# Layer 1's expert matrices: three certain blocks' loads go to other buffers, and the later blocks' places follow

## The chip, the core and the metric

The kernel runs on one core of a Trainium2 chip. The core has five engines with an instruction queue each: TensorE (PE, with its weight loads shown apart as PEld), VectorE (DVE), ScalarE (ACT), GpSimd (POOL) and SyncE (SP). 16 DMA engines move data between memory and the core's on-chip memory. The metric is device time in microseconds; the time before is the median of 8 runs, 1903.46 us (1897.4 to 1906.86).

## What is computed

Four layers over 2708 rows of 256 numbers. Each layer adds a product with the adjacency matrix, then a feed-forward part. The change lies in layer 1's feed-forward part, a mixture of 8 experts of which each row goes to one:

```python
H = gelu(layernorm(x) @ W1 + b1)            # 2708 x 1024
probs = softmax(H @ Wg + bg)                # 2708 x 8
assign = argmax(probs)
for e in range(8):
    y = H @ Wd[e] + bd[e]                   # 1024 x 256 matrix of the expert
    out += where(assign == e, probs[:, e] * y, 0)
x = x + out
```

## The kernel before

*Blocks.* Which expert a row goes to is known only on the chip. Rows of H are kept in memory (`hid`), and each row's number and weight are scattered to a place sorted by expert (`taken`). Every 128 places of one expert are a block. Layer 1 runs 24 blocks always, at positions 0 to 23. Positions 0 to 8 are the NA = 9 certain ones: blocks that are full by the first two of three groups of row tiles (2048 rows), taken in the order of the experts and run in thirds (0, 3, 6, 1, 4, 7, 2, 5, 8). Positions 9 to 23 are the ALWAYS = 15 rest blocks, in the order of the list REST1, whose pairs are (block of the rest, buffer). Should the data need more, a branch after position 17 (L1467, `all_again`) computes them; with these inputs its body isn't run, but every engine passes the branch.

*One position* (`Units`, L687 to 830). POOL gathers the 128 names from `taken` (L551), then their rows of `hid` into one of four tiles `hs` (L693). PE turns the rows (L708, 8 transposes, through `ps_acc`), ACT copies them to `hTs` (L709), PE multiplies with the expert's matrix `wb` into `yacc` (L781, 16 instructions), DVE adds the bias, a part of `wb` too (L784), and scales (L785), and POOL scatters the rows to `given` (L537). PE turns the next position's rows ahead of a position's product. At the last certain position (8) it is otherwise: the transposes of position 9 stand two products before the end of position 8's, those of position 10 right behind them.

*Matrices.* A matrix with its bias is 128 x 2304 floats (1152 KB, `L1_ffn_Wdp`). `weights1` loads it through SP's queue into one of six buffers `wb`, numbered 0 to 5. SP first reads the block's expert from on-chip memory (L564). A buffer remembers the expert it was loaded with, and the load (L1170) carries a condition: it moves nothing if the expert is the same. The issue waits for the buffer's last reader, DVE's bias addition. SP works in order, so what is queued behind a waiting issue waits too. Buffers 0 to 2 lie in a pool of their own (`w1`); buffers 3 to 5 are in a pool (`w1r`) that opens when the gate's pool is closed, in its room. `fetch` keeps two matrices ahead for the certain positions; `fetch_rest` keeps up to three ahead for the rest, and asks for none whose buffer is still to be read.

Before, the certain positions use buffers 0, 1, 2 in turn (position b uses b % 3), and so the loads of positions 6, 7 and 8 follow the reads of positions 3, 4 and 5. The rest starts with buffers 3, 4 and 2.

*What comes behind.* The rows of `given` are read back by SP (`load_tiles`, L56) as `mine`, and added to x by DVE and POOL (L1587). Layer 2 begins with transposes (L1592), their copies (ACT, L1594) and a projection (L267). Its pool `t3` lies in the room of layer 1's, among it the constants that POOL loads (L127 Wr, L121, L1530, L1532, L1537). The builder orders each engine's instructions; waits follow from which tiles share room.

Of the kernel before, what the change touches and what calls it, by code (L numbers as in the profile page):

```python
# [49 lines left out]
def load_tiles(nc, dst, tiles, src, first=0):  # L50

    done = []
    full = [t for t in tiles if rows(t) == P]
    if full:
        t0, m = full[0], len(full)
        done.append(nc.sync.dma_start(  # L56
            dst[:, t0 - first : t0 - first + m, :],
            src[t0 * P : (t0 + m) * P, :].rearrange("(t p) d -> p t d", p=P)))
    for t in tiles:
        if rows(t) < P:  # L60
            done.append(nc.sync.dma_start(dst[: rows(t), t - first, :],
                                          src[t * P : t * P + rows(t), :]))
    return done
# [3 lines left out]
def adj_ffn4(ctx: ExitStack, tc: tile.TileContext, a: dict, out: bass.AP):  # L67
# [64 lines left out]
    def pin(last=None):  # L132

        pinned.append(tc.keep_in_program_order(
            s.preload_act_table_set("natural_log_exp_and_others")))
        if last is not None:
            tc.add_manual_dep(pinned[-1].ins, last, mybir.DependencyInfo(
                mybir.DependencyClass.NoSync, mybir.DependencyReason.DATA), reason="table")
# [405 lines left out]
    def behind(i, past):  # L544
        for p in past:
            tc.add_manual_dep(i.ins, p.name, mybir.DependencyInfo(
                mybir.DependencyClass.Sync, mybir.DependencyReason.DATA), reason="scattered rows")
# [114 lines left out]
    class Units(Blocks):  # L662
# [72 lines left out]
        def fetch_rest(self):  # L735
            while self.rest and len(self.rest_ahead) < 3:
                n, k = self.border + self.at[1], REST1[self.at[1]][1]
                if max((i for i in range(n) if buffer_of(i) == k), default=-1) >= self.now:
                    break
                self.rest_ahead.append(self.weights(self.border + self.at[1], expert_of(self.rest.pop(0))))  # L740
                self.at[1] += 1
# [128 lines left out]
    NA, MOST = 9, (2 * N + E * (P - 1)) // (2 * P)  # L870
# [5 lines left out]
    with ExitStack() as l0:  # L876
# [99 lines left out]
        for tiles in GROUPS:  # L976
# [8 lines left out]
            for j in range(FULL):  # L985
# [50 lines left out]
                if end and j == 0:  # L1036
                    items = [(early, b, past0, taken[0][: 2 * held0], True) for b in range(N0)]
# [12 lines left out]
            if end:  # L1050
# [3 lines left out]
                hc = l0.enter_context(  # L1054
                    tc.tile_pool(name="c0", side="right", reuse_waits="tile", bufs=1))
# [61 lines left out]
        for q, t0, t1 in ((P, 0, FULL), (LAST, FULL, NT)):  # L1117
            d = ps_tmp()
            for t in range(t0, t1):
# [16 lines left out]
    NA, MOST = 9, (N - E) // P + E + 1  # L1136
    assert NA <= -(-(held - E * (P - 1)) // P)
    ALWAYS, AHEAD1 = 15, 9
    EARLY, prepared = GROUPS1[0], {}

    REST1 = [(0, 3), (4, 4), (6, 2), (1, 3), (5, 4), (7, 2), (2, 3), (8, 2), (3, 3),
             (9, 5), (10, 1), (11, 4), (12, 0), (14, 2), (13, 0)]

    def buffer_of(b):

        return b % 3 if b < NA else REST1[b - NA][1]

    assert sorted(b for b, _ in REST1) == list(range(ALWAYS))
    assert all(b < AHEAD1 for b, _ in REST1[:AHEAD1])
    with ExitStack() as l1:  # L1150
# [5 lines left out]
        wbs, reads = {}, []  # L1156
# [5 lines left out]
        def weights1(b, e):  # L1162

            k = buffer_of(b)
            if k not in wbs:
                wbs[k] = [wbs["pool" if k < 3 else "more"].tile([P, 2048 + D], F32, name="wb", bufs=3),
                          None]
            wb, was = wbs[k]
            wbs[k][1] = e
            i = nc.sync.dma_start(wb, a["L1_ffn_Wdp"][bass.ds(e, 1)].rearrange("e p n -> p (e n)"),  # L1170
                                  cond=None if was is None else e != was)
            after(i, reads[-1])
            return wb.rearrange("p (f d) -> p f d", d=D)
# [180 lines left out]
        work1 = Units(hw, given[1], weights1, hid)  # L1354
        for tiles in GROUPS1:
# [83 lines left out]
            if end:  # L1439
                sums.close()  # L1440
                gnn.close()
                psum_pool(l1, 3, 3)
                wbs["pool"] = l1.enter_context(
                    tc.tile_pool(name="w1", side="right", reuse_waits="tile", bufs=1))
                hc = l1.enter_context(
                    tc.tile_pool(name="c1", side="right", reuse_waits="tile", bufs=1))
                work1.hs.append(hc.tile([P, HC * P], F32, name="hs", bufs=1))
                work1.hTs = [hc.tile([P, HC, P], F32, name="hTs", bufs=2) for _ in range(2)]
                g.memset(work1.hs[-1], 0.0)
                work1.more()  # L1450
                between = work1.pieces(hc, lambda b: beside(b), {NA + AHEAD1: lambda: branch()})
                send1(tiles, ready, between)
                break
# [9 lines left out]
        items = [(rest, b, past, taken[1], False) for b in range(MOST - NA)]  # L1463

        def branch():

            with tc.If(left[0] > 0):  # L1467
                work1.all_again(hc, items[AHEAD1:], wbs[3][0],
                                slice(NA + AHEAD1, NA + ALWAYS))
            pin(scattered["given1"][-1].name)  # L1470
            wbs[3][1] = None
            known_rows = list(scattered["given1"])
            for t0, o in zip(EARLY[::4], work1.early):
                for i in load_tiles(nc, o.rearrange("p (t d) -> p t d", d=D), range(t0, t0 + 4),
                                    given[1], t0):
                    tc.declare_no_dep(i.ins, group="given1", keep=known_rows,
                                      reason="rows of other blocks")
                    tc.add_to_no_dep_group("given1read", i.ins)
                    behind(i, known_rows)
# [6 lines left out]

        work1.add([items[b] for b, _ in REST1])
        for _ in between:
# [799 lines left out]
```

## Time and profile before

| what | us |
|---|---|
| median of 8 runs (lowest, highest) | 1903.46 (1897.4, 1906.86) |
| the profiled execution's own time | 1902.83 |
| its span, first to last instruction | 1901.1 |
| DVE busy | 1075.0 |
| ACT busy | 656.9 |
| POOL busy | 390.7 |
| first product of layer 1's blocks (L781) | 961.4 |
| end of the last one | 1088.3 |

The mean granted TensorE clock of the execution is 0.985. A line of the timeline has the start, the span, the engine, the line, the operation, what is written and read, the shape and the count; in brackets stands the idle time of the engine just before it and what ended that. "issue" means that the engine waited for nothing that the profile shows; "PEq" is PE's own instruction queue. In the table of windows the times are those from the span's start.

### The profile page before, as it was taken

To read this page: it belongs to the slowest core of one execution; us is meant where nothing else is said; L and a number is where in the kernel's file an instruction comes from. 1 tells how busy PE (TensorE), PEld (TensorE's weight loads), DVE (VectorE), ACT (ScalarE), POOL (GpSimd) and SP (SyncE) were. 2 spreads that over 40 slices of the span, in tenths; PEclk is the share of its full clock that TensorE was granted. 3 is DMA by queue.
4 is the path that set the end of the run, shared out by engine and by line. 5 is a ranking of instruction groups with operands and counts; after the bars stand their busy time and mean duration, and the time that the engine had idled before them with its cause. 6 is when DMAs were issued, how large, how long until landed. Compare 5 with 4: busy or idle time off the path is not lost. (4 is left out here: it accounts for less than half of the span.)

```text
span 1901.1 us, 25846 instructions
## 1 busy us (share of the span) xinstructions
PE 1820.5 (96%) x9453; PEld 1332.0 (70%) x9453; DVE 1075.0 (57%) x2467; ACT 656.9 (35%) x1472; POOL 390.7 (21%) x460
## 2 busy tenths in 40 slices
PE   8999998999999999999888999999899999999998
PEld 7888777888888788888777878887566733233344
DVE  7686871443433625344542365555355498888877
ACT  8777741222222302113222332322232542132232
POOL 0015353333322001403446410000000100011020
PEclk9999998999998999999989999999899999999999
DMA  8536655887773554544746452000101000012120
GB/s 267 158 99 165 228 187 210 333 333 265 289 285 101 178 151 124 126 131 122 220 134 220 171 94 18 1 1 1 44 1 34 18 1 23 23 26 37 23 37 18
DMA packets 92638, 232.81 MB, mean 122 GB/s; under 512 B 18223, under 2 KB 48983, under 8 KB 84952
## 3 DMA queue, kind: packets, MB, share of 16 engines
q1 hardware_dynamic: 70936, 184.46, 30.3%
q0 software_dynamic: 21568, 46.61, 9.0%
q8 instruction: 78, 1.28, 0.3%
q14 instruction: 56, 0.46, 0.1%
HBM read 218.39 MB, written 30.80 MB: 131 GB/s over the span
## 5 line engine op out<-in xcount | busy, mean ns | idle before, releaser
L2160 DVE SCALAR_TENSOR_TENSOR e<-arena,G,mask 128x1024 f32<-128x1024 f32 (+1 forms) x252 | 275.1, 1150 | 34.1 <-PE den L2197 33.2
L2189 PE MATMUL num<-e,wh 128*64 128x512 f32 (+4 forms) x1056 | 214.0, 549 | 0.7 <-ACT L_gnn_W L1498 0.3
L1420 PE MATMUL acc<-sup,adrow 128*128 128x256 f32 x882 | 198.5, 382 | 3.5 <-DMA adrow<-in_adjT 1.9
L1723 PE MATMUL ps_acc<-hh,e 128*128 128x257 f32 x882 | 199.2, 382 | 1.7 <-ACT o L1666 1.7
L1024 PE MATMUL acc<-msg,wt 128*128 128x256 f32 x882 | 197.9, 381 | 1.8 <-DVE wt L974 1.2
L1420 PEld LDWEIGHTS acc<-sup,adrow 128*128 128x128 f32 x882 | 164.9, 190 | 31.7 <-issue 5.5
L1024 PEld LDWEIGHTS acc<-msg,wt 128*128 128x128 f32 x882 | 165.0, 190 | 27.6 <-issue 2.1
L1723 PEld LDWEIGHTS ps_acc<-hh,e 128*128 128x128 f32 x882 | 163.7, 190 | 29.2 <-ACT o L1666 4.3
L649 PE MATMUL yacc<-wb,hTs 128*128 128x256 f32 x736 | 170.8, 384 | 6.7 <-DVE ys L651 4.0
L615 PE MATMUL ps_acc<-xTs,wa 128*128 128x256 f32 (+1 forms) x768 | 170.3, 374 | 4.2 <-DVE xTs L605 3.0
L617 ACT ACTIVATE hTs<-ps_acc,wa 128x256 f32<-128x256 f32 (+1 forms) x192 | 88.8, 465 | 247.3 <-PE yacc L649 167.1
L615 PEld LDWEIGHTS ps_acc<-xTs,wa 128*128 128x128 f32 x768 | 136.8, 190 | 31.1 <-DVE xTs L605 6.2
L649 PEld LDWEIGHTS yacc<-wb,hTs 128*128 128x128 f32 x736 | 138.5, 192 | 26.0 <-DVE ys L651 5.1
L2189 PEld LDWEIGHTS num<-e,wh 128*64 128x64 f32 (+1 forms) x1056 | 70.0, 136 | 122.8 <-issue 104.9
L1715 DVE SCALAR_TENSOR_TENSOR e<-Rb,G,mask 128x640 f32<-128x640 f32 (+2 forms) x110 | 85.0, 774 | 90.5 <-PE ps_acc L1723 90.4
L2197 PE MATMUL den<-e,wh 128*32 128x512 f32 (+4 forms) x1056 | 112.2, 545 | 0.0
L1385 DVE TENSOR_SCALAR mask<-adrow 128x1024 uint8<-128x1024 f32 (+1 forms) x66 | 41.3, 625 | 123.4 <-DMA adrow<-in_adjT 123.2
L221 ACT COPY xT<-ps_tmp 128x256 f32<-128x256 f32 x76 | 26.9, 367 | 199.9 <-PE ps_tmp L220 199.5
L781 PE MATMUL yacc<-wb,hTs 128*128 128x256 f32 x384 | 91.0, 392 | 0.6 <-DMA wb<-in_L_ffn_Wdp 0.6
L974 DVE SCALAR_TENSOR_TENSOR wt<-adrow,wt 128x640 f32<-128x640 f32 (+3 forms) x67 | 71.0, 1063 | 25.8 <-ACT wt L141 24.5
L2197 PEld LDWEIGHTS den<-e,wh 128*32 128x32 f32 (+1 forms) x1056 | 33.0, 109 | 73.7 <-issue 69.6
L537 POOL DMA_INDIRECT given<-ys,xs x46 | 65.4, 1423 | 92.0 <-DVE ys L652 77.9
(487 smaller groups left out, 2631.6 us busy)
## 6 DMA issues: line engine op xcount, KB each, us to landing
adhalf<-in_adjT SPq DMA_DIRECT2D x42, 677.0 KB
wb<-in_L_ffn_W2p SPq DMA_DIRECT2D x24, 1152.0 KB
wb<-in_L_ffn_Wdp SPq DMA_DIRECT2D x24, 1152.0 KB
wa<-in_L_ffn_W1b SPq DMA_DIRECT2D x24, 1028.0 KB
adrow<-in_adjT SPq DMA_DIRECT2D x42, 512.0 KB
adrow<-in_adjT SPq DMA_DIRECT2D x42, 320.0 KB
adrow<-in_adjT SPq DMA_DIRECT2D x21, 576.0 KB
adrow<-in_adjT SPq DMA_DIRECT2D x21, 448.0 KB
```

Source lines behind the costliest of these rows:

```text
L615: i = te.matmul(p[:, f % 2, : m * P], lhsT=w1[:, c, f * P : (f + 1) * P], rhs=xT[:, c, : m * P], start=(c == 0), stop=(c == DC - 1))
L617: s.activation(hT[:, f, : m * P], p[:, f % 2, : m * P], AF.Gelu, bias=bias[:, f : f + 1])
L649: te.matmul(q[:, k, :], lhsT=hT[:, f, k * P : (k + 1) * P], rhs=w2[:, f, :], start=(f == 0), stop=(f == HC - 1))
L781: te.matmul(q, lhsT=hT[:, f, :], rhs=w2[:, f, :], start=(f == 0), stop=(f == HC - 1))
L974: v.scalar_tensor_tensor(wt, ad, 1.0, wt, op0=ALU.is_lt, op1=ALU.mult)
L1024: te.matmul(p[:q, n - pair[0], :], lhsT=wt[:, k : k + q], rhs=msg[:r, j, :], start=(j == 0 and n == pair[0]), stop=(j == FULL - 1 and n == ...
L1420: te.matmul(p[:q, n - pair[0], :], lhsT=ad[:, k : k + q], rhs=sup[:, jj, :], start=(jj == 0 and n == pair[0]), stop=(jj == FULL - 1 and n ...
L1715: i = v.scalar_tensor_tensor(e[:r, :w], Rb[:r, c0 : c0 + w], G[:r, j, :], mask[:r, j, c0 : c0 + w], op0=ALU.max, op1=ALU.mult)
L1723: te.matmul(p[:, : D + 1], lhsT=e[:, k : k + q], rhs=hh[:, j, :], start=(j == 0), stop=False)
L2160: v.scalar_tensor_tensor(e[:, :w], slow[:, m % 2, k, :w], G[:, j, 2 * pair + k, :], mask[:, j, c0 : c0 + w], op0=ALU.max, op1=ALU.mult)
L2189: te.matmul(num[k * DK : (k + 1) * DK, hf, :q], lhsT=wh[some, j, 2 * pair + k, :DK], rhs=e[some, :q], start=(j == 0), stop=(j == FULL), ti ...
L2197: te.matmul(den[z * Q : (z + 1) * Q, :q], lhsT=wh[some, i, 2 * pair + k, DK : DK + 1] .to_broadcast([some.stop - some.start, Q]), rhs=e[so ...
```

## The change

Certain blocks 2, 5 and 8, which are run at positions 6, 7 and 8, get buffers 3, 4 and 5 in place of 0, 1 and 2. The list of the rest keeps its order of blocks and gets other buffers. The buffer that the branch's body overwrites is now 0 in place of 3.

```diff
-    REST1 = [(0, 3), (4, 4), (6, 2), (1, 3), (5, 4), (7, 2), (2, 3), (8, 2), (3, 3),
-             (9, 5), (10, 1), (11, 4), (12, 0), (14, 2), (13, 0)]
+    REST1 = [(0, 0), (4, 1), (6, 5), (1, 0), (5, 1), (7, 5), (2, 0), (8, 5), (3, 0),
+             (9, 2), (10, 4), (11, 1), (12, 3), (14, 5), (13, 3)]

     def buffer_of(b):

-        return b % 3 if b < NA else REST1[b - NA][1]
+        return (b % 3 if b < NA - 3 else b - NA + 6) if b < NA else REST1[b - NA][1]
...
-                work1.all_again(hc, items[AHEAD1:], wbs[3][0],
+                work1.all_again(hc, items[AHEAD1:], wbs[0][0],
                                 slice(NA + AHEAD1, NA + ALWAYS))
             pin(scattered["given1"][-1].name)
-            wbs[3][1] = None
+            wbs[0][1] = None
```

The first rest positions, 9 and 10, now use buffers 0 and 1, which positions 3 and 4 were the last to read; the last ones, 22 and 23, use 5 and 3 where they used 2 and 0. PE's and ACT's instructions keep their order. SP's keep theirs but for their targets, conditions and waits. On DVE a part of layer 2's first statistics, a memset (L1521) and a comparison (L1548) change places with the last two bias additions. On POOL the last but one scatter now stands ahead of the load of Wr (L127), the last scatter behind it, and the six loads L121 to L1537 behind that; before, all seven loads stood ahead of both scatters.

## The prediction

> **What bounds the kernel now.** The page's first part comes first: TensorE (PE) is busy in nearly the whole span, so a change of transfers can only win where PE stands still or runs at half clock. The table of windows over the end of layer 1 shows where that is (columns: the stretch and its span, busy us and instructions of PE, PEld, DVE, ACT and POOL, granted clock, busy share of the DMA engines, GB/s):
>
> ```profile
> PE 1820.5 (96%) x9453; PEld 1332.0 (70%) x9453; DVE 1075.0 (57%) x2467; ACT 656.9 (35%) x1472; POOL 390.7 (21%) x460
> ```
> ```profile
> 983.00:993.00 10.00, 9.46 (x35) 8.20 (x36) 1.33 (x5) 2.35 (x5) 5.56 (x6) 0.68 0.34 97
> 993.00:1015.00 22.00, 19.18 (x103) 16.30 (x101) 3.12 (x8) 3.22 (x6) 14.14 (x15) 1.00 0.98 376
> 1015.00:1052.00 37.00, 34.96 (x185) 30.80 (x186) 9.64 (x26) 9.85 (x18) 25.38 (x25) 0.95 0.43 131
> 1052.00:1062.00 10.00, 6.97 (x35) 5.88 (x34) 1.56 (x4) 2.46 (x3) 3.12 (x4) 0.96 0.84 320
> ```
>
> Two stretches have the DMA engines at 0.98 and 0.84, and PE loses 2.8 and 3.0 us in them; between 983 and 993 the engines are at 0.34. The timeline of PE tells what the first one costs:
>
> ```profile
> 1003.37 3.62 PE L781 MATMUL yacc<-wb,hTs 128*128 128x256 f32 x16
> 1007.55 2.83 PE L781 MATMUL yacc<-wb,hTs 128*128 128x256 f32 x12 [0.56 <-DMA wb<-in_L_ffn_Wdp]
> ...
> 1012.71 0.63 PE L708 MATMUL ps_acc<-ident,hs 128*128 128x128 f32 x4 [0.59 <-issue]
> 1016.77 1.12 PE L708 MATMUL ps_acc<-ident,hs 128*128 128x128 f32 x4 [3.43 <-issue]
> 1017.68 4.86 PE L781 MATMUL yacc<-wb,hTs 128*128 128x256 f32 x16
> ```
>
> One block's output (L781, x16) is position 7 at 1003.37, 8 at 1007.55, 9 at 1017.68. Undisturbed, the step is 4.33 us (999.04 to 1003.37). The next, position 10, begins at 1023.25, so three steps took 19.88 us in place of 12.99: 6.9 us are lost. Of these 0.56 + 0.59 + 3.43 = 4.58 us are gaps, and 4.86 - 3.62 = 1.24 us are the half clock that follows the last gap.
>
> Why there: the trace's packets of 9216 B (a matrix row) are 11 x 128 in this layer, so 11 of the 24 issues of L1170 move a matrix and 13 are skipped. Three come at 932 to 946, and five, of positions 6 to 10, lie end to end from 993.3 to 1014.5. The queue's own timeline has positions 6, 7 and 8 issued at 991.47, 994.93 and 998.82, each held by DVE's bias addition of position 3, 4 or 5, the last reader of the buffer it overwrites. Positions 9 and 10 follow at 1000.14 and 1001.58 into the two untouched buffers. Gathers of hidden rows issued inside that stretch land late: the one of 1001.35 after 1010.2, while that of 983.17 took until 987.6. PE's signals to the others are late there too: DVE begins the addition of position 7 at 1013.12, though PE's record of its last product ends at 1007.0; why, the trace doesn't say.
>
> **The change, part by part.**
>
> *Positions 6, 7, 8 into buffers 3, 4, 5 (moved).* The order of SP's instructions gives what each then waits for: the last gelu into the closed gates' room (ACT, over by 957.5), the stores of hidden rows (issued until 971.88, landed by 976) and older stores of POOL. All this is past when SP has issued position 5, at 981.12. I read the spacing of such issues, 0.9 us, off 931.23, 932.21, 933.05: the three go at about 982 to 984, 9 to 15 us sooner, into the stretch at 0.34. Positions 9 and 10 now overwrite buffers 0 and 1 and inherit the waits at 991.47 and 994.9, still 7 to 9 us sooner than before. The same five transfers then run from about 983 to 1005: 5 x 3.5 us (932.97 to 937.42 and its like) and some four gathers. Position 8 has its matrix before 997, not at 1007.5: the 0.56 us go. The place that is sensitive is the end of position 8, where the code puts two blocks' transposes back to back and PE needs ACT's copies at once; in steady step that place is at 1007 to 1012, after the stretch. Bounds: nothing (PE's signals to ACT come late for a reason that has nothing to do with these loads) and -6.9 us. I take -5.8 us, the 4.58 and the 1.24 that the timeline shows, since the waits end with the transfers (1014.5 and 1016.1) and gaps of the kind are absent from 1024 to 1050, where nothing but gathers moves.
>
> What is queued behind the waiting issues: on SP only later matrices and, from 1065, the loads of given rows; nobody before position 9 needs those. What the three early loads meet: the gathers of 983.17 and 989.93, for positions 7 and 8, whose transposes stand at 998 and 1002.5 and which landed at 987.6 and 994.2. They have 8 to 10 us of slack, against 3.5 us per matrix ahead of them: hidden, at most 1 us if not.
>
> A rule on the other side, beside the row of 0.34: the Trainium skill's "DMA: Bandwidth & Descriptors", section "Issuing engines are not separate DMA queues", says that transfers of all issuers run on the same 16 engines and interleave. By it the burst is only moved, and the sum of this part would be the 0.56 us alone; the row of 993 to 1015 agrees that gathers and loads slow each other (0.98), and the row of 983 to 993 says there is room.
>
> *One matrix found in place (removed).* From the reference and its inputs I worked out the rows of each expert. The nine certain blocks are of experts 0, 2, 4, 0, 2, 4, 1, 3, 5; position 18 needs expert 4, which now still lies in buffer 2: 10 transfers, not 11. It was the first of the two that fill 1052.1 to 1061.7 (8 x 0.35 us per engine, 3.5 to 4 us). In that stretch PE stands at the branch of L1467:
>
> ```profile
> 1054.97 3.62 PE L781 MATMUL yacc<-wb,hTs 128*128 128x256 f32 x16
> 1061.61 1.94 PE L708 MATMUL ps_acc<-ident,hs 128*128 128x128 f32 x8 [3.03 <-PEq L1467]
> ```
>
> PE's branch takes 6.11 us there and its code packet starts 3.7 us after it; at layer 0's branch (L658, DMA half idle) it takes 3.54 us. Bounds: nothing (the other transfer still runs, from 1053.9 on), and -4.5 us (the 3.03 gap, and 0.9 + 0.6 us of half clock in the 1.94 against 1.04 and the 4.22 against 3.62 after it). I take -1.5 us: half the gap for half the bytes, the nearer row being this branch, not layer 0's.
>
> *The end of the layer (moved).* The last positions now read buffers 5 and 3. The constants of layers 2 and 3 lie in that room, and the order of POOL's instructions shows what follows: the load of L_ffn_Wr waits for DVE's bias addition of the last block and stands ahead of the last scatter; six more loads come behind the scatter, where they were ahead of it.
>
> ```profile
> 1082.84 0.79 POOL L127 DMA_DIRECT2D L_ffn_Wr<-in_L_ffn_Wr  x1
> ...
> 1087.40 1.06 POOL L537 DMA_INDIRECT given<-xn,names  x1 [0.30 <-issue]
> 1089.47 1.03 POOL L537 DMA_INDIRECT given<-xn,names  x1 [1.02 <-DVE sc L1623]
> ```
> ```profile
> 1089.47 2.50 DMA given<-xn,names
> ...
> 1092.64 3.92 DMA mine<-given
> ```
>
> The second fence is the chain that ended last: this scatter and the load behind it are on the path, and PE waits 2.06 us for them at 1095.96. The bias addition ends 1088.79, so 0.79 us of Wr makes the scatter start at 1089.6 or later: +0.2 to +0.8, I take +0.4. The six loads (540 KB) then share the engines with 768 KB of given rows: nothing (the engines are at 0.38 from 1090 to 1117) to +4 us (512 KB took 3.92); I take nothing. ACT's first copies of layer 2 no longer wait for the last bias addition; that is worth under 0.3 us and lies before the same 2.06 us wait, so nothing. PE's order is unchanged.
>
> *Sum:* -5.8 - 1.5 + 0.4 = -6.9 us. Against the profiled execution's own 1902.83 us (span 1901.1) that is **1895.9**. The median of the runs shown is 1903.46, 0.6 above, inside their spread of 1897.4 to 1906.9.
>
> **The rivals.** About 0.2% (3.8 us) is what a measurement of this kernel can tell from no change.
>
> *A, the forecast:* from -10.8 (6.9 and 4.5 in full, +0.6) to -3.4 (the gaps go, the rest not, +1.2): 1892 to 1899.4. Chance 0.53.
>
> *B, the burst only moves.* PE's signals come late wherever matrices and gathers crowd, now at 990 to 1003; one block's slack of 3.6 us does not hide it. For it: at 993 to 1003 DMA already stood at 0.9 and more. Against: there PE lost nothing. -0.6 - 1.5 + 0.4 = -1.7: 1901.1, no change. 0.28.
>
> *C, it doesn't do what it says:* the three loads are still held (an old reader of the room that the order of instructions tells of, but late), and leave SP at 991 as before. Then +0.4 alone: 1903.2. 0.06.
>
> *D, slower, the end of the layer.* Wr ahead of the scatter (+0.8) and the six loads beside the given rows (+4) lengthen the wait of 2.06 us. It decides once the wait passes 2.7: the gap of 2.06 was followed by full clock, one of 2.72 at 289.2 by half clock, and the half clock after 3.43 us lasted 3.4 us, 1.7 lost. 0.8 + 4 + 1.7 = +6.5, with B's -2.1 for the loads: 1907.2. 0.13.
>
> A rule on the clock, in a sentence of its own: the Trainium skill's "TensorE: Matmul & The Clock Gate", "Part 1: The HAM clock gate", has the clock drop after an idle window of about 3.4 us; by it D's clock term would be nothing unless the wait nearly doubled, while the row of 2.72 us is below that.
>
> **How the numbers follow.** Forecast A, 1895.9. Faster is A: 0.53. Same is B and C: 0.34. Slower is D: 0.13. The range reaches from 1891.5 (A's low end) to 1904.5 (C and the noise of the runs): it leaves out D and a little of A.
>
> **What would show it.** Right: issues of L1170 for positions 6 to 8 at 982 to 984; no wait for wb at position 8; position 10 near 1016 to 1017 in place of 1023.25; 10 x 128 packets; a gap under 3 us at L1467; the last scatter under 1 us behind the last bias addition. Wrong: the gaps of 4.58 us at another place before 1010, or PE's wait for the given rows (the 2.06 us at 1095.96) above 2.7 us.

## The result, and the profile after

The kernel after takes 1914.15 us (median of 12 runs, 1911.13 to 1919.26), the kernel before 1904.15 us beside it (34 runs). The ratio is 1.0057, with a 95% interval of 1.0046 to 1.0068: slower by about 10 us, where 1895.9 us and a gain were forecast. The profiled execution has a span of 1910.4 us and an own time of 1912.2 us, against 1901.1 and 1902.8 before.

The transfers moved as the prediction said. The issues of positions 6, 7 and 8 stand at 980.64, 982.30 and 983.32, the five transfers run from 980.6 to 1000.0, and the layer has 10 x 128 packets of 9216 B. The table of windows of the kernel after shows it (columns as before):

```profile
983.00:993.00 10.00, 10.00 (x46) 8.83 (x46) 1.21 (x4) 2.01 (x4) 3.10 (x3) 0.84 1.00 411
993.00:1015.00 22.00, 20.58 (x111) 17.85 (x110) 3.46 (x9) 3.81 (x7) 13.83 (x14) 1.00 0.60 209
1015.00:1052.00 37.00, 28.09 (x141) 23.57 (x140) 8.08 (x22) 7.62 (x14) 24.85 (x25) 0.86 0.40 124
```

The DMA engines are full from 983 to 993 (1.00, 0.34 before) and at 0.60 after that (0.98 before). But PE's loss did not go. It lies between 1015 and 1052 now, 8.9 us of 37 against 2.0 before, where the DMA engines are only at 0.40. The timeline of PE shows the place:

```profile
1017.20 3.21 PE L781 MATMUL yacc<-wb,hTs 128*128 128x256 f32 x14
1021.62 0.59 PE L781 MATMUL yacc<-wb,hTs 128*128 128x256 f32 x2 [1.21 <-issue]
...
1023.03 0.27 PE L708 MATMUL ps_acc<-ident,hs 128*128 128x128 f32 x1 [0.70 <-issue]
1023.75 0.62 PE L708 MATMUL ps_acc<-ident,hs 128*128 128x128 f32 x2 [0.45 <-issue]
1030.13 1.11 PE L708 MATMUL ps_acc<-ident,hs 128*128 128x128 f32 x4 [5.76 <-ACT hTs L709]
```

Position 10 begins at 1017.20, 6 us ahead of before (1023.25), as forecast. Then come gaps of 1.21, 0.70, 0.45 and 5.76 us and half clock until 1034, and position 11 begins at 1031.03, 3.5 us behind before. ACT is idle in the 5.76 us: by PE's records the transposes it waits for are over at 1024.4, and ACT starts their copies at 1029.49. Such a late signal of PE is what the prediction had seen at 1013 and could not explain.

What stood still ahead of that is POOL. Its timeline in the kernel after (first fence), and its longest wait there in the kernel before (second):

```profile
983.20 1.04 POOL L693 DMA_INDIRECT hs<-hid,names  x1 [2.29 <-issue]
...
985.86 1.05 POOL L551 DMA_INDIRECT names<-taken,b_ix  x1 [0.31 <-issue]
995.87 1.02 POOL L693 DMA_INDIRECT hs<-hid,names  x1 [8.96 <-issue]
```
```profile
989.93 1.03 POOL L693 DMA_INDIRECT hs<-hid,names  x1 [3.04 <-PE yacc L781]
```

The gather of names issued at 985.86 lands at 994.2 in the trace's packets, behind the matrices; before, issued at 985.83, it had landed at 988.5. The gather of rows needs these names, and POOL works in order: it stands still for 8.96 us, and from 1002.46 to 1025.95 it runs 18 indirect transfers back to back.

At the end of the layer, before (first fence) and after (second; its last line is from the chain that ended last):

```profile
1095.96 0.63 PE L1592 MATMUL ps_tmp<-ident,x 128*128 128x128 f32 x4 [2.06 <-DVE x L1587]
...
1099.58 3.65 PE L267 MATMUL ps_acc<-w_l,xT 128*128 128x258 f32 x16
```
```profile
1092.85 0.76 POOL L127 DMA_DIRECT2D L_ffn_Wr<-in_L_ffn_Wr  x1 [2.70 <-ACT xT L1594]
1093.91 1.01 POOL L537 DMA_INDIRECT given<-xn,names  x1 [0.31 <-issue]
...
1099.90 0.63 PE L1592 MATMUL ps_tmp<-ident,x 128*128 128x128 f32 x4 [2.91 <-DVE x L1587]
...
1103.99 0.63 PE L1592 MATMUL ps_tmp<-ident,x 128*128 128x128 f32 x4 [1.72 <-DVE x L1587]
...
1105.31 0.69 PE L1592 MATMUL ps_tmp<-ident,x 128*128 128x128 f32 x4 [0.69 <-DVE mv L194]
...
1106.20 5.12 PE L267 MATMUL ps_acc<-w_l,xT 128*128 128x258 f32 x16
...
1096.65 6.48 DMA mine<-given
```

The wait of 2.06 us has become 2.91, waits of 1.72 and 0.69 us have joined it, and the 16 products that follow run in 5.12 instead of 3.65 us. The load of given rows on the chain of waits takes 6.48 us, 3.92 before.

Two stretches carry the comparison from here on. "Blocks" is the time from the layer's first L781 to the end of the last; "end" is from there to layer 2's first L1723. The difference of the two spans, +9.3 us, is -0.65 (the blocks start earlier) + 3.81 (blocks, 126.89 to 130.70) + 4.93 (end, 28.04 to 32.97) + 1.24 (all that comes behind; e10 and e15, which have the old end, show +1.6 to 1.7 there, so it is not counted to the change).

### The profile page after: what moved, and what is told of

It is laid out like the page before. It is cut to its first block, busy times and chain, and to the rows that moved or that the text cites. A ratio compares the mean times of both kernels' runs of the same rounds, so it can differ in the third digit from the quotient of the medians.

```text
span 1910.4 us, 25846 instructions
## 1 busy us (share of the span) xinstructions
PE 1821.6 (95%) x9453; PEld 1330.7 (70%) x9453; DVE 1074.1 (56%) x2467; ACT 655.4 (34%) x1472; POOL 388.3 (20%) x460
## 3 DMA queue, kind: packets, MB, share of 16 engines
q1 hardware_dynamic: 70792, 183.28, 29.5%
q8 instruction: 78, 1.28, 0.3%
## 5 line engine op out<-in xcount | busy, mean ns | idle before, releaser
L1723 PE MATMUL ps_acc<-hh,e 128*128 128x257 f32 x882 | 199.2, 382 | 1.7 <-ACT o L1666 1.7
L1723 PEld LDWEIGHTS ps_acc<-hh,e 128*128 128x128 f32 x882 | 163.7, 190 | 29.2 <-ACT o L1666 4.3
L2189 PEld LDWEIGHTS num<-e,wh 128*64 128x64 f32 (+1 forms) x1056 | 70.0, 136 | 122.8 <-issue 104.9
L781 PE MATMUL yacc<-wb,hTs 128*128 128x256 f32 x384 | 89.4, 387 | 1.2 <-issue 1.2
```

Source lines behind the costliest of these rows:

```text
L781: te.matmul(q, lhsT=hT[:, f, :], rhs=w2[:, f, :], start=(f == 0), stop=(f == HC - 1))
L1723: te.matmul(p[:, : D + 1], lhsT=e[:, k : k + q], rhs=hh[:, j, :], start=(j == 0), stop=False)
L2189: te.matmul(num[k * DK : (k + 1) * DK, hf, :q], lhsT=wh[some, j, 2 * pair + k, :DK], rhs=e[some, :q], start=(j == 0), stop=(j == FULL), ti ...
```

## The experiments

| run | kernel | blocks | end | ratio to before (95%) |
|---|---|---|---|---|
| | before / after | 126.9 / 130.7 | 28.0 / 33.0 | 1 / 1.0057 |
| e1 | after's front, before's end | 134.6 | 28.2 | 1.0044 (1.0028, 1.0059) |
| e2 | before's front, after's end | 128.5 | 32.6 | 1.0030 (1.0009, 1.0050) |
| e3 | after, constants later | 134.3 | 29.7 | 1.0048 (1.0034, 1.0062) |
| e5 | after, names 3 ahead | 117.0 | 30.6 | 0.9982 (0.9967, 0.9996) |
| e6 | before, names 3 ahead | 118.8 | 28.3 | 0.9954 (0.9937, 0.9972) |
| e7 | e1, names 3 ahead | 121.9 | 28.1 | 0.9978 (0.9964, 0.9993) |
| e17 | e3, names 3 ahead | 122.5 | 28.1 | 0.9978 (0.9962, 0.9993) |
| e10* | e6 and breaks on POOL | 114.3 | 28.5 | 0.9949 (0.9937, 0.9962) |
| e12* | e5, Wr behind the scatter | 114.1 | 29.5 | 0.9958 (0.9944, 0.9973) |
| e13* / e14* | before / after | 123.3 / 123.4 | 28.2 / 32.4 | 1 / 1.0025 (1.0013, 1.0036) |
| e15* | as e10 | 111.8 | 28.8 | 0.9953 (0.9939, 0.9966) |

Blocks and end, in us, are those of one profile each. The experiments ran on five chips, and their traces are of two kinds. In e1 to e8, e17 and e18, as in the two profiles above, PE's signals come late in places. In the runs with a star (and e9, e11, e16) the stall that this makes near 979 is absent: position 3 begins 16.1 us after the first product there, and 21.8 to 23.9 us after it in all the others but e18. The kernel before takes 1886.7 to 1889.1 us on these chips, not 1903.5 to 1905.1. Blocks and ratios are compared only within a kind. One profile's blocks are no exact measure: those of the kernel before are 126.9 us above and 123.7 in e8, which differs from it in layer 2 alone.

### The two halves alone: e1 and e2

```diff
 e1 (from after)
-             (9, 2), (10, 4), (11, 1), (12, 3), (14, 5), (13, 3)]
+             (9, 2), (10, 4), (11, 1), (12, 0), (14, 2), (13, 0)]
 e2 (from before)
-             (9, 5), (10, 1), (11, 4), (12, 0), (14, 2), (13, 0)]
+             (9, 5), (10, 1), (11, 4), (12, 0), (14, 5), (13, 3)]
```

> Change: positions 6 to 8 use buffers 3 to 5 as in the kernel after, but the last three positions use buffers 0, 2 and 0 as before; POOL's order is then that of before (all seven constant loads ahead of both last scatters), and one more matrix is loaded (11). Theory 1 (the end of the layer is lengthened by the constants' loads, +4.9 us from the last product to layer 2's first product of L1723: 40.04 against 35.11): that stretch is 35 to 35.5 again. The front (+3.2 us at the last product in the profile after) is then all that is left: +3 us, about 1907, if the PE stall at 1020 to 1030 belongs to the new places of the transfers; -6 to -7, about 1897, if that stall was an accident of one execution. Rival (the end was longer because the front shifted it, not because of POOL's order): the stretch stays at about 40 and the time at about 1914.

> Change: the kernel before with only its last two positions moved to buffers 5 and 3, which gives POOL the order of the kernel after (Wr ahead of the last scatter, six loads behind it) and one transfer more (12). Theory 1 (the end alone costs 4.9 us): last product's start at about 1081 as before, 40 us from there to the first product of L1723, time about +5, 1909. Rival (the end needs the front's shift): 35 to 36 us for that stretch and a time within 1 us of before, 1904 to 1905.

Both halves lose. e1 has the old end (28.2) and still costs 8.0 us in the medians (1913.01 against 1905.02), where I had expected 3; its blocks are 7.7 us longer, so the stall was no accident of one execution. e2 has the old front and the end of after (32.6), with the same waits of PE (3.06, 1.23 and 0.69 us), and costs 4.2 us. The end theory stands. The front, from which everything was hoped, costs at least as much.

### The constants: e3

```diff
-        wr = mat(tp, "L2_ffn_Wr", E)
-        ...   (six more loads)
+        wr = tp.tile([P, DC, E], F32, name="L2_ffn_Wr", bufs=1)
+        ...   (tiles only; the seven loads behind the loop that adds the given rows)
```

> Change: the kernel after, with its seven loads of the constants of layers 2 and 3 put behind POOL's last addition of given rows, so that nothing stands ahead of the last scatter and nothing shares the DMA engines with the given rows. Theory 1 (Wr's load holds the last scatter by about 1.3 us, the six others stretch the load of given rows from 3.9 to 6.5 us): the stretch from the last product to the first of L1723 falls from 40.04 to 34 to 35.5 us, the given rows land in 4 us, and the time falls by 5 to 6 us to about 1908 to 1909. Rival (the given rows are slow for another reason): the stretch stays above 39 us and the time at 1913 to 1915.

The end falls to 29.7, in the terms of the expectation to 36.8 us from 40.04. That is most of the way, but not the 34 to 35.5 that I had named: the last scatter starts 0.67 us behind the bias addition as before, yet PE's wait for the given rows is 2.56 us and half clock follows it (eight products of L267 in 3.35 us, 1.91 before). In e17, which has the same end, the wait is 2.03 us, no half clock follows, and the end is 28.1. With the constants' loads out of the way the loss goes, then, but for a half clock that falls there in some profiles; those of e4 and e8, with the old end, have it too, and ends of 29.3 and 29.2. The time hardly follows: its blocks are like those of e1, and between 1.0048 and 1.0057 the intervals cannot tell 3 us. The profile after, from which I counted, has the shortest blocks of the three with this front.

### Without the transfers: e4

```diff
-                                  cond=None if was is None else e != was)
+                                  cond=None if was is None else e > E if 6 <= b <= 11 else e != was)
```

(with buffers 0 to 2 for positions 6 to 11).

> Change: the conditions of the loads for positions 6 to 11 are made false and these positions use buffers 0 to 2, so the five transfers between 980 and 1015 are left out and these blocks are computed with matrices of other experts. Theory A (the five transfers cause the PE stalls with late signals, at 1007 to 1016 before and at 1020 to 1031 after): between 990 and 1040 PE has no gap over 1 us and no half clock, one position takes 4.3 us, position 11 begins 30 us after position 4. Theory B (the stalls have a cause outside these transfers, such as POOL's back-to-back gathers and scatters or PE's own instruction supply): a stall of 3 to 6 us with a burst of late signals is still there somewhere between 1000 and 1035.

Theory A falls as it was stated. No matrix moves between 975 and 1050, and PE's timeline with those of DVE and ACT still has this:

```profile
998.86 3.62 PE L781 MATMUL yacc<-wb,hTs 128*128 128x256 f32 x16
1000.31 0.42 DVE L784 TENSOR_TENSOR xn<-yacc,wb 128x256 f32<-128x256 f32 x1 [5.64 <-PE ps_acc L708]
...
1003.20 0.59 ACT L709 COPY hTs<-ps_acc 128x512 f32<-128x512 f32 x1 [7.78 <-PE yacc L781]
1003.84 2.86 PE L781 MATMUL yacc<-wb,hTs 128*128 128x256 f32 x12 [1.37 <-ACT hTs L709]
```

The transposes that ACT copies at 1003.20 ended at 998.6 by PE's record. Signals come late without any transfer of a matrix. But the transfers are not innocent of the time: from position 4 to position 11 takes 32.6 us here, 36.8 in the kernel before and 42.2 in the kernel after, where seven steps of 4.33 us would be 30.3. By what way they cost it, the next three runs show.

### The names: e5, e6, e7

```diff
-            while self.names_todo and len(self.named) < (3 if self.places[1] >= self.border else 1):
+            while self.names_todo and len(self.named) < 3:
```

> Change: the kernel after, with POOL gathering the names (L551) up to three positions ahead for the certain positions too, where it kept one ahead; no names gather is then in flight while the matrices of positions 6 to 8 are. Theory N (POOL's wait for the names: in the profile after, the names gather of 985.86 took until 994.2 behind the three early matrices, where before it was down at 988.5, and POOL, in order, stood still for 8.96 us ahead of the gather of rows at 995.87; after that it ran back to back until 1026 and PE got rows and signals late): POOL has no wait over 4 us between 983 and 1000, and the stretch from the first product to the end of the last falls from 130.7 to 134.6 us (three profiles with these buffers) to about 125 to 127; the end of the layer keeps its +4.9. Time about 1914 - 6 = 1908. Rival S (PE's late signals come from something else and stay): the stretch stays at 130 or more and the time within 2 us of 1914.

> Change: the kernel before, with the same three names ahead. Theory N: POOL's waits ahead of the row gathers at 989.93 (3.04 us) and 997.41 (2.51 us) go; the PE stall at 1007 to 1017 gets shorter by up to 4 us. Time 1900 to 1904. Rival S: nothing changes in PE's gaps, time within 1.5 us of before.

> Change: positions 6 to 8 in buffers 3 to 5 as after, the last positions in buffers 0 and 2 as before (POOL's order at the end as before), and three names ahead. Theory N with the end's theory: neither loss is there, the stretch from first product to the last one's end is about 125 us against 126.9 before, the end 28 us; time 1898 to 1903, at or below before. Rival S: as the run with these buffers and one name ahead, 134.6 us for the stretch and 1913.

In e5 the names of positions 6 to 8 are there before the matrices move, and the blocks are 117.0 us, shorter by 14 to 18 than in the three profiles with this front and one name ahead; I had expected 125 to 127. What I wrote of names in flight was wrong in one point: those of the first rest blocks still are, and one wait over 4 us is left on POOL:

```profile
989.51 1.00 POOL L693 DMA_INDIRECT hs<-hid,names  x1 [4.62 <-PE ps_acc L708]
```

The three gathers before it land between 986.2 and 989.5, in the same stretch of the matrices, but only this one wait comes of it, in place of 2.29 and 8.96 us.

e6, three names ahead without the change, is the fastest of this kind of chip: 1894.58 us against 1903.48, and it gains more than the 1900 to 1904 that I had given it. The kernel before waited for names too: its row gathers at 983.17, 989.93 and 997.41 idle for 1.69, 3.04 and 2.51 us and start 0.4 to 1.4 us after the last packet of their names. With names ahead the front of after costs 3.5 us between e7 and e6 (1898.08 and 1894.58), 8.0 without (e1 against before). The medians alone do not settle how much of the loss the names carry, as the intervals are wide and those of e6 and e7 overlap. The profiles say where it sits. From position 4 to position 11, on chips with late signals:

| kernels | us |
|---|---|
| front of before, one name ahead (before, e2, e8) | 36.8, 37.5, 35.9 |
| front of after, one name ahead (after, e1, e3) | 42.2, 43.0, 41.8 |
| front of before, three names ahead (e6) | 31.8 |
| front of after, three names ahead (e5, e7, e17) | 32.0, 31.9, 31.6 |
| after's order, no transfer there (e4) | 32.6 |

So the early transfers cost some 5.6 us in this stretch with one name ahead and nothing with three; and with three, neither front is worse off than with no transfers at all. What is left between the blocks of e7 and e6 lies behind it, nearly all in one wait of PE (e7; none in e6):

```profile
1032.43 1.14 PE L252 MATMUL ps_tmp<-w_l,all_ones 128*128 128x258 f32 x4 [3.03 <-DVE w_l L277]
```

DVE had begun the bias addition ahead of L277 late, at 1029.24. e5, with the same front, has no wait there.

### What makes the signals late: e8, e9, e16, e18

```diff
+            burst = hp.tile([P, 20, 2], F32, name="bu", bufs=1)
+            for k in range(20):
+                g.indirect_dma_start(out=burst[:, k, :], out_offset=None, in_=taken[1],
+                                     in_offset=bass.IndirectOffsetOnAxis(ap=bx[:, 0:1], axis=0), ...)
 e9, e16, e18: besides, ahead of every fourth
+                if k % 4 == 0 and k:
+                    after(g.memset(pause, 0.0), last)
```

> Change: the kernel before with 20 gathers of 128 rows of 8 bytes added on POOL, back to back (about 26 us), in layer 2's feed-forward part near 1360 to 1390, where POOL is idle, no one needs the gathered rows, and PE signals ACT every 1.7 us or DVE every 3.4 us. Theory P (a run of back-to-back indirect transfers on POOL is enough to hold PE's signals): in these 26 us DVE or ACT start over 3 us after PE's last product of a group, PE has gaps of 2 us or more that the kernel before has not, and they end 1 to 2 us after the last gather's issue; time +3 us or more. Rival (it takes more than POOL's run alone): the products of L375 and L1932 go on at 13.8 us per group as in the kernel before, time within 2 us of before.

The run of POOL from 1345.24 to 1369.78 is enough, in a place where the DMA engines are at 0.02. PE and DVE in e8:

```profile
1356.41 12.60 PE L1943 MATMUL ps_acc<-w,hT 128*128 128x256 f32 x57
1360.89 0.48 DVE L1945 SCALAR_TENSOR_TENSOR y<-x,mrs,ps_acc 128x256 f32<-128x256 f32 x1 [14.15 <-PE ps_acc L1943]
...
1369.36 0.90 PE L1943 MATMUL ps_acc<-w,hT 128*128 128x256 f32 x3 [0.35 <-issue]
...
1372.16 0.81 PE L1943 MATMUL ps_acc<-w,hT 128*128 128x256 f32 x3 [1.02 <-issue]
1372.21 0.48 DVE L1945 SCALAR_TENSOR_TENSOR y<-x,mrs,ps_acc 128x256 f32<-128x256 f32 x1 [9.63 <-remote]
```

The second group of 16 products is over at 1363.5 by PE's record, and DVE takes it up at 1372.21, 8.7 us late and 2.4 us after POOL's last issue. PE itself gets stuck (0.35 and 1.02, and 0.51 between them) as in the layer-1 stalls. In the kernel before, the 64 products run in one piece of 13.98 us. The time of this one execution, 1903.57, does not show it: the stretch from the first L1723 to the end is 4.6 us longer than in the kernel before, but the blocks of this profile happen to be 3.2 us shorter (123.7) and begin 1.8 us earlier.

> Change: the 20 added gathers in layer 2's feed-forward part again, with a POOL memset of 128x1024 (about 1 us) after every fourth. Theory P (PE's signals are held while POOL issues indirect transfers without a break, and come through at a break of about 1 us): no signal of PE is more than 2 us late between 1345 and 1385, the products of the second output group take 14 us without issue gaps as in the kernel before, though POOL's run is 4 us longer. Rival Q (the number of transfers in flight or the traffic is what holds them): DVE's first addition is again some 8 us late and PE has issue gaps of 0.4 to 1 us before the run ends.

> Twenty added gathers in layer 2 with a 1 us memset after every fourth, again. On a chip with late signals: theory P expects no signal over 2 us late between 1345 and 1385, rival Q one some 8 us late with issue gaps of PE as without the pauses. On a chip without them: nothing late, as in the run before.

Both ran on chips without late signals: nothing late, with or without breaks, though POOL runs 40 transfers in a row from 992 to 1045 there. They tell nothing of the breaks, but a run of POOL alone is not enough on every chip.

> The kernel before with three names ahead, the two POOL additions among the six scatters into taken, and in layer 2 the 20 added gathers with a 1 us memset after every fourth. On a chip with late signals: theory P expects the gap near 979 under 2 us and no signal over 2 us late between 1330 and 1370; rival Q expects the gap at 4 to 5 us and one signal some 8 us late in layer 2. On a chip without late signals it tells nothing new: nothing late.

e18 ran on a chip with late signals, and both signs that theory P named are there. In layer 2:

```profile
1355.25 13.98 PE L1955 MATMUL ps_acc<-w,hT 128*128 128x256 f32 x64
```

No piece is broken off, and no signal is late there. In the layer-1 blocks, the gap that e6 has (first fence) is gone in e18 (second fence):

```profile
979.19 1.97 PE L708 MATMUL ps_acc<-ident,hs 128*128 128x128 f32 x8 [4.46 <-ACT hTs L709]
```
```profile
975.59 2.48 PE L708 MATMUL ps_acc<-ident,hs 128*128 128x128 f32 x20
977.90 7.07 PE L781 MATMUL yacc<-wb,hTs 128*128 128x256 f32 x32
...
987.56 2.64 PE L781 MATMUL yacc<-wb,hTs 128*128 128x256 f32 x11 [2.14 <-issue]
```

Position 5 begins 25.74 us after the first product, 29.94 in e6. But the gain does not last: in the next long run of POOL (ten transfers to 988.5) PE has the gap of 2.14 us at 987.56, others follow, position 9 begins 49.0 us after the first product against 49.2 in e6, and the blocks end at 118.5, like e6's 118.8. The breaks moved the stall; that they remove it is shown for layer 2 alone, by one profile.

### Breaks among the six scatters: e10 and e15

```diff
                 scatter(taken[1], ix[:r, i, :], names[:r, i, :], N - 1, "taken1")
+                if ready is not None and i in (0, 2):
+                    after(g.tensor_tensor(pause, pause, pause, ALU.add), scattered["taken1"][-1].name)
```

> Change: the kernel before with three names ahead, and two POOL additions of 128x256 (0.6 us each) put after the first and the third of the six scatters into taken at 966 to 975, so that the run of ten back-to-back transfers there is broken into runs of 4, 2 and 5. Theory P: the gap of 4.46 us before the transposes at 979 (present in every kernel so far) shrinks to under 2 us and the half clock behind it goes; 3 to 5 us less than with names ahead alone (1894.6), so 1890 to 1892. Rival Q: the gap stays at 4 to 5 us and POOL's 2 us more cost 0 to +2: 1894 to 1897.

> Three names ahead and two POOL additions between the six scatters into taken, again. On a chip with late signals: theory P (a break of about 1 us lets PE's signals through) expects the gap of 4.46 us before the transposes near 979 to shrink below 2 us and a time 3 to 5 us under the 0.9954 of before that three names ahead alone had, ratio 0.993 to 0.994; rival Q expects the gap to stay and a ratio of 0.995 to 0.997. On a chip without them: ratio 0.9949 again.

Both on chips without late signals, where the gap near 979 isn't there in any kernel: 0.9949 and 0.9953, much like names ahead alone on the other kind of chip (0.9954). From position 4 to position 11 takes 33.9 and 33.6 us in them, and 41.7 to 42.9 in e9, e13 and e16, which have the same front and one name ahead on such chips. Names ahead alone was not run on this kind, so what the breaks cost or gain here stays open. Names ahead is what the faster versions share: e5, e6, e7, e10, e12, e15 and e17 all have it and all have intervals below 1, and no version without it has.

### After and before where no signal is late: e13, e14, e11

> The kernel before, unchanged, for a profile from the same chip as the three runs beside it. If the chip is of the kind of e1 to e8: first to last product's end 124 to 128 us, gaps of 4 to 7 us at 983 and of 3 to 6 us in all between 1003 and 1030, 1903 to 1905 us. If it is of the kind of e9 to e12: no late signals, 115 to 120 us, 1889.

> The kernel after, unchanged. Names chain (the names gather behind the three early matrices holds POOL by about 9 us, and PE then waits for rows or for signals) plus the end of the layer: on a chip of either kind POOL has a wait of 7 to 10 us ahead of one gather of rows between 983 and 1000, the stretch from the first product to the last one's end is 4 to 8 us longer than in the kernel before on that chip, the end 4 to 5 us longer, ratio 1.004 to 1.007. If the loss of the front needs the late signals, then on a chip without them the front is within 1 us of before and the ratio is 1.002 to 1.003 from the end alone.

e14 is slower by 0.25%, about half of the loss on the other chips, and by the two profiles it is the end alone: 32.4 against 28.2 us. The blocks are equal (123.4, 123.3; 122.8 and 124.6 in e9 and e16, which have the front of before). The front still changes where PE waits; PE's waits for rows in e13 (first fence) and e14 (second):

```profile
980.44 1.06 PE L708 MATMUL ps_acc<-ident,hs 128*128 128x128 f32 x8 [3.45 <-DMA hs<-hid,names]
990.91 1.11 PE L708 MATMUL ps_acc<-ident,hs 128*128 128x128 f32 x8 [4.26 <-DMA hs<-hid,names]
...
1046.24 1.79 PE L708 MATMUL ps_acc<-ident,hs 128*128 128x128 f32 x8 [4.33 <-DMA given<-xn,names]
```
```profile
989.49 1.94 PE L708 MATMUL ps_acc<-ident,hs 128*128 128x128 f32 x8 [9.95 <-DMA hs<-hid,names]
...
1048.96 1.81 PE L708 MATMUL ps_acc<-ident,hs 128*128 128x128 f32 x8 [2.57 <-PEq L1467]
```

There, too, the names stand behind matrices in both kernels. POOL waits 2.51, 4.44 and 5.67 us ahead of three gathers of rows in e13, and 6.18 and 7.65 us ahead of two in e14. (The profile puts these waits down to PE; but each ends 0.9 to 1.5 us after the last packet of the names, and PE is itself waiting for the rows.) The burst moved, and so did the wait. Up to position 12 e14 is 2.1 us behind; at the branch it makes 1.8 us good (4.33 to 2.57).

```diff
 e11 (from after)
             self.places[1] += 1
+            if 10 <= self.places[1] <= 16:
+                self.rows.append((m, h))
+                return
             i = g.indirect_dma_start(out=h, out_offset=None, in_=self.hidden[:n, :],
```

> Change: the kernel after without the row gathers (L693) of positions 9 to 15, whose products then use the rows that lie in the buffers already. POOL has two transfers per position in place of three from 1000 on, and PE waits for no rows there. Theory P in its place: POOL's run of 18 from 1002 to 1026 breaks up, no signal of PE is over 2 us late between 1000 and 1050, positions 10 to 16 take 6 x 4.33 = 26 us plus what stands there for other reasons (38.3 in the profile after, 27.8 before). POOL's wait of 9 us for the names ahead of the rows of position 8 stays, as it is not touched. Rival (the lateness belongs to PE or to the transfers of matrices): signals 3 to 8 us late are there between 1000 and 1050 as in the other kernels.

The chip shows no late signals at all, so this does not test theory P. POOL waits 6.44 and 7.31 us ahead of the two gathers that are left, PE 10.04 us for the rows, and positions 10 to 16 then take 27.3 us, close to six undisturbed steps (27.3 in e14 too, which has all the gathers). The wait for names is thus a loss by itself, without any help of late signals.

### Both costs removed: e12 and e17

```diff
 e12 (from e5)
-                tc.add_manual_dep(i, work1.at_end, mybir.DependencyInfo(
+                tc.add_manual_dep(i, scattered["given1"][-1].name, mybir.DependencyInfo(
 e17: the edit of e3 and that of e5
```

> Change: the kernel after with three names ahead, and the load of Wr behind the last scatter with the six others, so that only the sharing of the DMA engines by the six loads is left of the end's change. Theory 1a (Wr's load ahead of the scatter is worth 1.1 us and the rest is sharing): the last scatter starts under 0.7 us after the last bias addition, the stretch from the last product's end to the first of L1723 is 29.3 to 30.5 us against 30.6 with Wr ahead and 28.1 with the order of before; time 0 to 2 us below the 1900.7 of that kernel. Theory 1b (the scatter's delay takes PE's wait over the length after which half clock follows, and that is most of it): the stretch is 28 to 28.5 us and the time 2 to 3 us below.

In e12 the last scatter starts 0.68 us after the last bias addition (1.96 in the kernel after), and the end is 29.5 us against 30.6 in e5 with Wr ahead and 28.1 in e17 with nothing ahead or beside: within theory 1a's range. It does not decide for 1a: 1.5 us of the 29.5 are the half clock behind PE's wait of 2.31 us (eight products of L267 in 3.44 us), and the old end has come to 29.2 to 29.4 with it (e4, e8, e16, e18). The time cannot be compared with e5's, as the kinds of chip differ.

> The kernel after with three names ahead and with the seven loads of constants behind POOL's last addition of given rows: both costs that were found are removed. If the early transfers are worth what was predicted for them (the 0.56 to 1.4 us wait for wb at position 8 gone, one matrix fewer), the ratio to before is 0.992 to 0.9945, at least 1 us under the 0.9954 of three names ahead without the change; if they are worth nothing, 0.995 to 0.996; if they cost something besides, above that.

0.9978 (0.9962 to 0.9993): if the early transfers were worth what was forecast, 0.9945 or less was due, and 0.995 to 0.996 if they were worth nothing. They gain nothing, then, and rather lose some 4 us against e6. The blocks (122.5 against 118.8) lose it behind position 11, most of it in the place of e7's wait: PE stands 2.48 us ahead of L252, and DVE's bias addition there had begun late, at 1030.82. Why the late signal falls there in e7 and e17 and not in e5 and e6 stays open.

## Why the prediction was wrong

*The burst (-5.8 us forecast; +3.8 in the profile after, +7.7 in the blocks of e1).* The issues at about 982 to 984 and position 10 at 1017 were right, and the transfers ended at 1000, 5 us sooner than forecast. Two steps were wrong. The first is "They have 8 to 10 us of slack, against 3.5 us per matrix ahead of them: hidden, at most 1 us if not". That was worked out for gathers of rows only. Ahead of each stands a gather of names that it needs, on an engine that works in order, and with one name ahead the two latencies add. The rows were in the profile: L693 at 983.17, 989.93 and 997.41, idle for 1.69, 3.04 and 2.51 us. POOL's three issues per position take 3 x 1.32 = 3.96 us of PE's 4.33, so 0.37 us per position is all it has to make 8.96 us good. With three names ahead the loss of this front between positions 4 and 11 is gone (31.6 to 32.0 us, against 41.8 to 43.0). The second is "the waits end with the transfers (1014.5 and 1016.1)" as the reason to take -5.8, as if nothing but the transfers' place made the waits. Without the transfers the stretch is indeed shorter by 4.2 us than before (e4), but the way is by POOL: the gathers of names wait wherever the matrices stand, and POOL then catches up in one long run. Late signals need no transfer (e4, and e8 beside idle DMA engines), and in the kernel after they come in and behind POOL's run of 18, up to 1029.5, long after the transfers.

*The rule of the skill* that was weighed beside this, the section "Issuing engines are not separate DMA queues" of the Trainium skill's "DMA: Bandwidth & Descriptors", by which transfers of all issuers interleave on the same engines, was the better guide. The names gather of 8.4 us behind SP's matrices (2.7 before), issued by POOL, agrees with it, and B, its rival, holds for e14's blocks (123.4 and 123.3).

*No wait for wb at position 8 (0.56 us).* Right: none stands in the timeline, and e6, without the change, has one of 1.41 us there.

*One matrix in place (-1.5 us).* Ten transfers, as forecast. The gap at the branch did not shrink in the first pair (3.03 to 3.17 us), only the half clock behind it went: from position 16 to 18 it takes 11.59 us, 12.27 before. On the other kind of chip it went from 4.33 to 2.57 us, and the stretch from 13.43 to 11.69. So -0.7 and -1.7 in these two pairs. Over all profiles the stretch takes 10.7 to 12.6 us with ten matrices (seven, mean 11.5) and 10.9 to 13.4 with eleven (ten, mean 12.4): the sum's term was of the right order, and single profiles do not show more.

*The end (+0.4 us forecast, +4.9 in the profile after, +4.2 in the time of e2).* Rival D's mechanism, at 0.13, was what happened here. Five profiles with this order (after, e2, e5, e11, e14) have ends of 30.2 to 33.0 us, and twelve with the old one 28.0 to 29.4. Wr ahead of the scatter costs 1.28 us, not 0.4: besides its own 0.76 us it starts only 0.9 us behind the bias addition. The six loads, "I take nothing", stretch the load of given rows by 2.56 us (6.48 against 3.92), with the DMA engines at 0.96 from 1100 to 1104; the share of 0.38 that I averaged from 1090 to 1117 hid that the engines are needed in just those 4 us. As PE sees it: 3.26 us more of waits and 1.47 us of half clock. D's 6.5 was too much. Its "decides once the wait passes 2.7" was wrong: behind the wait of 2.91 us the clock held, half clock began at 1105.75, behind the shorter waits of 1.72 and 0.69, and in other profiles it follows a wait of 2.0 (the last section has the rows).

*The rivals.* D's time, 1907.2, was below the result for want of the front's loss, which no rival had.

## What to carry to other kernels

Before you move a load forward into a quiet stretch of the DMA engines, list the small dependent transfers there, the index behind which another gather waits, and ask how many of them their in-order engine has ahead: here two more steps of lookahead for a few bytes were worth 9 us, and the move of five matrices gained nothing with them and lost time without. A share averaged over 27 us says nothing of the 4 us in which a load on the path runs. And two things that end together in one profile may be tied by a third: here the small gathers that stood behind the large transfers, which moved with them.

## What the runs showed of the hardware that was not expected

- On three of the five chips, PE's signals come late by 2 to 9 us in and just behind long back-to-back runs of indirect transfers on POOL. e8 makes it happen with 20 gathers of 8 bytes a row beside idle DMA engines (share 0.02), where a signal is 8.7 us late and comes 2.4 us after the run's end; with a break of about 1 us after every four nothing is late there (e18, one profile). On two chips runs of 40 leave PE undisturbed, and the same kernel is about 0.9% faster there. What differs between the chips, and by what way POOL holds PE, stays open.
- The record of an indirect transfer on POOL is 1.0 us long whether its data land 2.7 us (before) or 8.4 us (after) after its start. The Trainium skill's "Perfetto Trace Analysis", section "DMA Instruction — SWDGE (GPSIMD)", says that this record ends when the descriptors are made, not when the data have moved; these two gathers agree.
- The length of PE's wait for the given rows did not decide whether half clock followed it. Behind waits of 2.00 us (e16), 2.05 (e4), 2.31 (e12), 2.56 (e3) and 2.63 (e5) the eight products of L267 took 3.26 to 3.58 us; behind 2.06 (before), 2.30 (e1) and 2.91 (after) they took 1.91. What decides it, no run here shows.
